# Gram products in three steps with sums of their own, the small chain moved behind them, and layer 3's first chunk prepared at a quarter's end

## The chip, the cores and the metric

The program runs on one core of a Trainium2 chip. A core has five engines with a queue of instructions each: TensorE (PE, matrix products; PEld is its loading of weights), VectorE (DVE), ScalarE (ACT), GpSimd (POOL) and SyncE (SP, which here only issues transfers). Data sits in SBUF (on chip, 128 partitions), products land in PSUM, and transfers (DMA) move tiles from and to memory. The metric is the device time of one execution in microseconds; before the change it is 2779.62 us in the median of three runs (2778.86 to 2781.19).

## The reference, cut to what matters

The input x has 16 images of 64 channels and 128 x 128 pixels. Four layers follow each other. Each normalizes its input by groups of two channels (`_gn`), computes something of it, and adds that to its unnormalized input.

```python
x = x + L0(_gn(x))   # gram = xf xf^T / N of an image; conv_w (gram xf)
x = x + L1(_gn(x))   # |Scharr x| + |Scharr y|, a channel at a time
x = x + L2(_gn(x))   # temporal shift of channels, then a 3x3 convolution and a bias
x = x + L3(_gn(x))   # 3x3 convolution, 1x1 convolution, batch norm over ALL images, leaky relu, clip to 0..255
```

Layer 0 needs the gram matrix of a whole image (64 x 64 sums over 16,384 pixels, and the sums of the channels) before it can give the first pixel. Its result is a single 64 x 64 matrix for each image, by which x is multiplied. The statistics of layer 1's normalization follow from the same gram matrix. Layers 2 and 3 need the mean and variance of the whole image that the layer ahead has made. Layer 3's batch norm needs all 16 images, so the end of the program reads everything once more.

## The kernel before, in words

Two halves of an image (64 rows each) lie on partitions 0 to 63 and 64 to 127, or, from layer 2 on, even and odd rows. An image is worked on in `NS` = 8 chunks of 8 rows, and a chunk of each stage is done in one *step*. The loop at line 1022 goes over steps, and each step over four quarters q = 0 to 3. Every engine works through its queue in the program's order (`InOrder`, line 56), so the order of this Python code is the order of the queues.

Four stages work at the same time, on different images:

- `Gram` (line 458) loads x of an image in eight pieces `xr` (line 493), copies each on ScalarE into the transposed layout `xw` (`rows_to_columns`, line 415), and then has TensorE multiply 128 pairs of columns (`gram_product`, line 406). `xw` has one buffer. For images 7 to 15 the products' sums `pg` lie in a part of `bank`, the PSUM bank that the small products of the chains use as well.
- `gram_chain` (line 303) turns the sums into layer 0's matrix `abd` and into the coefficients `co1` of layer 1's normalization. It is a generator: some sixteen links, alternately small products on TensorE and small operations on VectorE, and two square roots on ScalarE (`sd`). `tick` (line 256) is called at the end of each quarter and advances each open chain by a link. `coefficients` (line 279) is a shorter chain of the same kind, which gives the normalization of layers 2 (`coefs2`) and 3 (`coefs3`).
- `Front` (line 520) does layers 0 and 1: `po` is the product of x with `abd`, `xh` the normalized rows, `u` and `e` the Scharr filters on VectorE, whose absolute values ScalarE takes at the start of quarter 2.
- `Layer2` (line 736) normalizes its chunk `v` in quarter 1 on ScalarE; GpSimd then scales edges and zeroes columns (six instructions); VectorE makes differences `d` of rows, GpSimd issues transfers that copy them into `qd`; TensorE multiplies `one` and `two`. ScalarE copies `one` into `c`.
- `Layer3` (line 884) does the same for layer 3, with `prepare` (line 890) for the normalization. For chunk 0 `prepare` first takes the coefficients, has VectorE make two small factors for the chunk's first and last row (`edge_lower`, `edge_upper`), and then has ScalarE normalize a row with `edge_lower` and the chunk's two halves. Before, it is called in quarter 1 in the stage's own turn (line 941), and that turn is the first of the three stages'.

Image b enters `Front` with chunk 0 in step 15 + 8b, `Layer2` in 25 + 8b, `Layer3` in 35 + 8b. For b = 7 to 15 `Gram` begins at step 8b - 19. Its products were issued in quarters 0 and 2 of step 8b - 11 and in quarter 0 of 8b - 10, 44, 42 and 42 of them. In a steady loop the steps repeat every eight, so the number of a step modulo 8 tells what it holds: chunk 0 of layer 3 is prepared in step 34 + 8b (2 modulo 8), the chain ran from step 6 over 7, 0, 1 to 2.

At the end of each step, in quarter 3, the loop calls `Layer2` once more with "last of 3" (line 1038), where the difference for the next chunk is made. After the loop, a tail reads y and x of all images, applies the batch norm and writes the result.

Of the kernel before, what the change touches and what calls it, by code (L numbers as in the profile page):

```python
# [10 lines left out]
F32 = mybir.dt.float32  # L11
AF = mybir.ActivationFunctionType
ALU = mybir.AluOpType
# [3 lines left out]
P = 128  # L17
# [91 lines left out]
def tile_kernel(ctx: ExitStack, tc: tile.TileContext, x, cw_h, w2_t, b2, wbin_t, w1_t, b1, gamma, beta, consts, out):  # L109
# [141 lines left out]
                    )  # L251


    chains = []

    def tick():
# [45 lines left out]

    def gram_chain(b, pg):

        gs = stp.tile([P, C + 1], F32, tag="gs", name=f"gs_{b}", bufs=1)
        dve.tensor_copy(gs, pg)
        if b > 1:
            yield
        gd = sm(C + 1)
        small_product(gd, k("same"), gs)  # L310
        yield
        g = stp.tile([P, C + 1], F32, tag="g", name=f"g_{b}", bufs=1)
        dve.tensor_scalar_mul(g, gd, 1.0 / HW)
        mu = g[:, C:C + 1]
        st = sv("st0", 2)
        dve.tensor_copy(st[:, 0:1], mu)

        junk0 = stp.tile([P, C], F32, tag="junk0", name=f"junk0_{b}", bufs=1)
        dve.scalar_tensor_tensor(
            junk0, g[:, 0:C], GN_EPS, k("Id"), op0=ALU.add, op1=ALU.mult, accum_out=st[:, 1:2]  # L320
        )
        if b > 1:
            yield
        pm = sm(2)
        small_product(pm, k("gavg"), st)
        yield
        r, me = sv("r"), sv("me", 2)
        yield from rstd(pm, r, me)

        vv = sv("vv", 3)  # L330
        dve.tensor_copy(vv[:, 0:1], mu)
        dve.tensor_sub(vv[:, 1:2], mu, me[:, 0:1])
        dve.tensor_scalar_mul(vv[:, 2:3], me[:, 0:1], -1.0)
        dd = stp.tile([P, 2, C], F32, tag="dd", name=f"dd_{b}", bufs=1)
        for s in range(2):
            dve.tensor_scalar_mul(dd[:, s, :], k("Id"), vv[:, s:s + 1])
        if b > 1:
            yield

        pr = sm(2 * C)  # L340
        small_product(pr, k("all"), dd.rearrange("p s c -> p (s c)"))
        yield

        t0 = stp.tile([P, C], F32, tag="t0", name=f"t0_{b}", bufs=1)
        dve.scalar_tensor_tensor(t0, pr[:, 0:C], vv[:, 0:1], g[:, 0:C], op0=ALU.mult, op1=ALU.subtract)
        cs = stp.tile([P, 2, C], F32, tag="cs", name=f"cs_{b}", bufs=1)
        for s in range(2):
            dve.scalar_tensor_tensor(cs[:, s, :], pr[:, C:2 * C], vv[:, 1:2], t0, op0=ALU.mult, op1=ALU.subtract)
        rc = stp.tile([P, C], F32, tag="rc", name=f"rc_{b}", bufs=1)
        dve.tensor_scalar(rc, cwh, r, 0.5, op0=ALU.mult, op1=ALU.mult)  # L350
        csf = cs.rearrange("p s c -> p (s c)")
        if b > 1:
            yield
        pq = sm(C)
        small_product(pq, csf, rc)
        yield
        r2 = sv("r2")
        dve.tensor_mul(r2, r, r)
        for s in range(2):
            rows = slice(s * C, (s + 1) * C)  # L360
            dve.tensor_scalar_mul(wbd[rows, rows], pq[rows], r2[rows])
        ad = stp.tile([P, C], F32, tag="ad", name=f"ad_{b}", bufs=1)
        dve.scalar_tensor_tensor(ad, pq, r2, k("Id"), op0=ALU.mult, op1=ALU.add)
        abd = stp.tile([P, P], F32, tag="abd", name=f"abd_{b}", bufs=EARLY + 3)
        dve.tensor_add(abd, wbd, k("I"))
        if b > 1:
            yield
        pd = sm(C + 3)
        small_product(pd[:, 0:C], csf, ad)
        small_product(pd[:, C:C + 2], abd, vv[:, 0:2])  # L370
        small_product(pd[:, C + 2:C + 3], wbd, vv[:, 2:3])
        yield
        pp = stp.tile([P, 2, C], F32, tag="pp", name=f"pp_{b}", bufs=1)
        dve.tensor_mul(
            pp, pd[:, 0:C].unsqueeze(1).to_broadcast([P, 2, C]), ad.unsqueeze(1).to_broadcast([P, 2, C])
        )
        av = sv("av", 3)
        dve.tensor_copy(av, pd[:, C:C + 3])
        if b > 1:
            yield  # L380
        pk = sm(1)
        small_product(pk, pp.rearrange("p s c -> p (s c)"), k("q"))
        if b > 1:
            yield
        bias = av[:, 2:3]
        st1 = sv("st1", 2)
        dve.tensor_add(st1[:, 0:1], av[:, 0:1], bias)
        t = sv("t1")
        dve.scalar_tensor_tensor(t, av[:, 1:2], av[:, 1:2], pk, op0=ALU.mult, op1=ALU.subtract)
        dve.scalar_tensor_tensor(  # L390
            st1[:, 1:2], st1[:, 0:1], st1[:, 0:1], t, op0=ALU.mult, op1=ALU.subtract
        )
        if b > 1:
            yield
        pm = sm(2)
        small_product(pm, k("gavg"), st1)
        yield

        co = stp.tile([P, 5], F32, tag="co1", name=f"co1_{b}", bufs=EARLY + 3)
        r, mean = co[:, 0:1], co[:, 3:4]  # L400
        yield from rstd(pm, r, co[:, 3:5], GN_EPS)
        dve.scalar_tensor_tensor(co[:, 1:2], bias, mean, r, op0=ALU.subtract, op1=ALU.mult)
        dve.reciprocal(co[:, 2:3], r)
        lead[b] = abd, co

    def gram_product(pg, w):

        s = w % 2
        pe.matmul(
            pg[s * C:(s + 1) * C, :], xw[:, w // 2, 0:C, s], xw[:, w // 2, :, s],  # L410
            start=(w < 2), stop=(w >= W - 2),
        )
        last[0] = s

# [8 lines left out]
    def first_gram():  # L423
# [13 lines left out]
        for m in range(NS + 1):  # L437
            if m < NS:
                two = ps_two.tile([P, 2, CP, W], F32, tag="two", name=f"turned_{m}").rearrange("p a j w -> p (a j) w")
                for j in range(R):  # L440
                    pe.transpose(two[:, j], src[m][:, j * P:(j + 1) * P], k("I"))
                for h, copy in ((0, dve.tensor_copy), (1, act.copy)):
                    copy(xw[:, m * R:(m + 1) * R, 0:C, h], two[:, :, h * C:(h + 1) * C])
            if m > 0:
                for w in range(2 * R * (m - 1), 2 * R * m):
                    gram_product(pg, w)
        run(Front, 0, Front.first, 0)
        live[Front, 0].load(1)

# [6 lines left out]
                rows_to_columns(1, link - 2, rows[link - 2])  # L456

    class Gram:
        first, last = 0, NS + 1

        def __init__(self, b):
            self.b, self.xr, self.w = b, {}, 0

        def at(self, i, q):
            b = self.b
            if i < NS:
                if q == 0 and i != 1:
                    for m in range(i + (1 if i == 2 else 2) if i else 0, min(i + 3, NS)):
                        self.load(m)

                if q == 3 and i > 0:
                    for m in (0, 1) if i == 1 else (i,):
                        rows_to_columns(b, m, self.xr.pop(m))
                return
            n = 4 * (i - NS) + q

            self.part({0: 44, 2: 42, 4: 42}.get(n, 0))
            if n == 6:
                chains.append(gram_chain(b, self.pg))

        def part(self, n):
            if self.w == 0 and n:
                if self.b <= 2 * EARLY:
                    self.pg = ps_g.tile([P, CP, W], F32, tag="g", name=f"pg_{self.b}")[:, 0, 0:C + 1]
                else:

                    self.pg = bank[:, 3 * P:3 * P + C + 1]
            for _ in range(n // 2):
                for s in (1 - last[0], last[0]):
                    gram_product(self.pg, self.w + s)  # L490
                self.w += 2

        def load(self, m):
# [390 lines left out]
    class Layer3:  # L884
# [37 lines left out]
        def at(self, i, q):  # L922
# [10 lines left out]
            if q == 1:  # L933
                if 0 <= i < NS:
# [2 lines left out]
                    self.v.pop(i)  # L937
                    self.c = ring.tile([P, CP * W], F32, tag="c3", name=f"c3_{b}_{i}", bufs=1)
                    act.activation(self.c, flat(one), AF.Identity, bias=b1_sb)
                if i + 1 < NS:  # L940
                    self.prepare(i + 1)
                if 1 <= i:
                    y = self.y.pop(i - 1)
# [4 lines left out]
            if q == 2:  # L948
                if 0 <= i < NS:
# [5 lines left out]
                        self.c.unsqueeze(1).to_broadcast([P, 2, CP * W]),  # L955
                        op0=ALU.mult, op1=ALU.add, accum_out=bn_sum[:, n:n + 1],
                    )
                if i + 1 < NS:
                    difference("d3", 0, self.v[i + 1])
            if q == 3:  # L960
                if i + 1 < NS:
                    self.twin(0)
                    difference("d3", 1, self.v[i + 1])
                if 0 <= i < NS:
                    act.activation(
                        junk, self.y[i].rearrange("p s j w -> p (s j w)"), AF.Square,
                        accum_out=bn_sq[:, n:n + 1],
                    )
# [51 lines left out]
            fetched[0] += 1  # L1020

    for step in range(starts[2][1] - 2, steps):
        for q in range(4):
            for b in range(B):

# [5 lines left out]
            for stage, at in starts:  # L1031
                if stage is Front and q in (1, 3):
                    issue_rest()
                for b in range(B):
                    run(stage, b, step - at - NS * b, q)
            if q == 3:
                for b in range(B):
                    run(Layer2, b, step - starts[1][1] - NS * b, "last of 3")
            for b in range(1, B):
                at, n = pace[b]  # L1040
                if n == 1:
# [113 lines left out]
```

## Time and profile before

| What | Value |
|---|---|
| Median of three runs | 2779.62 us |
| The profiled execution | 2778.27 us |
| Its span in the profile | 2776.5 us |
| PE busy | 2175.3 us, 78% |
| DVE busy | 2192.0 us, 79% |
| ACT busy | 2112.6 us, 76% |
| POOL busy | 893.2 us, 32% |
| Gram products into `bank` (xw), 2304 matmul rows | 76.5 us |
| Columns, `xw<-xr` on ScalarE, 120 | 139.7 us, 1178 ns each |

Busy time of an engine is the time in which it ran something, not time without which the program would be shorter. "<-" after a row names what ended the idle time before it. In the names, what is written stands left of "<-" and what is read right of it. All instructions that go through `InOrder` carry one line (L73), so groups are told apart by tiles. A float32 matmul appears as two rows of the trace, and a pair that works on both column halves of the array as four. The page cuts the span into forty slices; in the digits 9 means 90% or more.

### The profile page before, as it was taken

Reading aid. Unit: us, or ns where it says so; the run is one execution under the profiler, and the core shown is the slowest. Engines: PE = TensorE matmul, PEld = TensorE weight load, DVE = VectorE, ACT = ScalarE, POOL = GpSimd, SP = SyncE. Lnnn points to the kernel's source line nnn. Section 1 sums busy time; section 2 is a strip of 40 time slices with the busy share of each in tenths; the row PEclk is TensorE's granted clock in tenths of the full one; section 3 lists DMA queues with packets and bytes.
Section 4 is the critical chain, followed back from the end, with each engine's and each line's share of the span. In section 5 each row is a group of like instructions: output and inputs, shape, how many; then the busy total and the mean of one; then the engine's idle time right before and its main releaser. Section 6 shows DMA issues by size and latency. Waiting matters only on the chain. (4 is left out here: it accounts for less than half of the span.)

```text
span 2776.5 us, 46105 instructions
## 1 busy us (share of the span) xinstructions
PE 2175.3 (78%) x14804; PEld 886.4 (32%) x14804; DVE 2192.0 (79%) x3623; ACT 2112.6 (76%) x3177; POOL 893.2 (32%) x1350
## 2 busy tenths in 40 slices
PE   6578899999999999999999999999999994000000
PEld 4233433434343434343433342333334641000000
DVE  4999999898989898989899999999996435333332
ACT  4766889898989898989898988999997667333332
POOL 2055434343434343434343344444444300000000
PEclk8689999999999999999999999999999997555555
DMA  8799888988888888888888777878877768999999
GB/s 205 201 229 238 211 216 226 231 215 229 218 227 213 229 221 221 216 230 216 230 218 227 206 188 197 217 202 219 215 199 195 213 196 288 420 420 420 420 420 384
DMA packets 693601, 685.96 MB, mean 247 GB/s; under 512 B 60096, under 2 KB 580448, under 8 KB 693360
## 3 DMA queue, kind: packets, MB, share of 16 engines
q1 hardware_dynamic: 668208, 613.83, 75.2%
q0 software_dynamic: 25152, 69.18, 10.2%
q8 instruction: 119, 1.95, 0.3%
q14 instruction: 122, 1.00, 0.1%
HBM read 346.23 MB, written 268.44 MB: 221 GB/s over the span
## 5 line engine op out<-in xcount | busy, mean ns | idle before, releaser
L73 PE MATMUL two<-d,w 128*64 128x508 f32 (+2 forms) x2560 | 846.8, 588 | 0.0
L73 PE MATMUL two<-d,wi 128*64 128x508 f32 (+3 forms) x1536 | 578.0, 579 | 0.0
L73 POOL DMA_DIRECT2D qd<-d x512 | 270.8, 531 | 903.7 <-DVE d L73 287.4
L73 PE MATMUL two<-qd,pk 128*64 128x512 f32 (+1 forms) x1024 | 519.0, 588 | 13.3 <-DMA qd<-d 12.5
L73 POOL TENSOR_SCALAR edges<-v,co 64x8 f32<-64x8 f32 x512 | 359.9, 703 | 307.7 <-ACT v L73 231.4
L73 DVE TENSOR_TENSOR d<-v 128x512 f32<-128x512 f32 (+1 forms) x512 | 345.6, 678 | 87.6 <-issue 55.5
L73 PE MATMUL one<-v,w 128*64 128x508 f32 (+2 forms) x1600 | 378.6, 599 | 34.8 <-ACT c L73 34.8
L73 PEld LDWEIGHTS two<-d,w 128*64 128x64 f32 x2560 | 263.1, 136 | 314.9 <-issue 278.5
L73 PE MATMUL one<-v,wi 128*64 128x508 f32 (+3 forms) x1536 | 358.5, 599 | 3.1 <-issue 2.6
L73 ACT COPY qd<-d 64x512 f32<-64x512 f32 x512 | 315.4, 616 | 20.8 <-DVE d L73 14.5
L73 DVE SCALAR_TENSOR_TENSOR e<-e 128x1032 f32<-128x1032 f32 (+1 forms) x256 | 312.9, 1222 | 0.0
L73 ACT ACTIVATE xh<-po,co 128x128 f32<-128x128 f32 (+1 forms) x480 | 275.2, 621 | 31.4 <-PE po L73 22.7
L73 POOL TENSOR_SCALAR v<-v,kc 128x9 f32<-128x9 f32 x256 | 234.6, 930 | 12.0
L73 DVE SCALAR_TENSOR_TENSOR y<-two,c 128x1024 f32<-128x1024 f32 x128 | 155.9, 1218 | 102.8 <-ACT v L73 65.4
L73 PEld LDWEIGHTS two<-d,wi 128*64 128x64 f32 x1536 | 175.6, 136 | 186.0 <-issue 169.6
L73 ACT ACTIVATE v<-x,co 128x512 f32<-128x512 f32 (+2 forms) x368 | 234.9, 705 | 0.0
L73 ACT ACTIVATE u<-u 128x1024 f32<-128x1024 f32 x128 | 135.3, 1057 | 106.8 <-DVE u L73 106.4
L73 PE MATMUL po<-x,abd 64*64 64x512 f32 (+1 forms) x1024 | 178.5, 643 | 44.0 <-ACT xh L73 41.0
L73 PEld LDWEIGHTS one<-v,w 128*64 128x64 f32 x1600 | 126.0, 139 | 237.9 <-issue 162.7
L73 PEld LDWEIGHTS two<-qd,pk 128*64 128x64 f32 x1024 | 136.3, 136 | 153.9 <-issue 110.6
L73 PEld LDWEIGHTS one<-v,wi 128*64 128x64 f32 x1536 | 108.9, 138 | 224.1 <-issue 209.0
L73 DVE SCALAR_TENSOR_TENSOR u<-xh 128x1170 f32<-128x1170 f32 x128 | 175.6, 1371 | 5.1 <-ACT xh L73 4.2
(165 smaller groups left out, 3333.9 us busy)
## 6 DMA issues: line engine op xcount, KB each, us to landing
x<-in_x SPq DMA_DIRECT2D x256, 256.0 KB, 4.1
x_d<-u SPq DMA_DIRECT2D x512, 128.0 KB, 3.8
y_d<-y SPq DMA_DIRECT2D x512, 128.0 KB, 4.0
x_d<-x SPq DMA_DIRECT2D x496, 128.0 KB, 2.6
xr<-in_x SPq DMA_DIRECT2D x120, 512.0 KB, 6.4
qd<-d POOLq DMA_DIRECT2D x256, 130.0 KB, 3.1
qd<-d POOLq DMA_DIRECT2D x256, 129.8 KB, 3.9
v<-x_d SPq DMA_DIRECT2D x448, 72.1 KB, 3.3
```

The costliest lines, as they stand in the source:

```text
L73: return self.tc.keep_in_program_order(call(*args, **kwargs))
```

## The change

Three things are edited.

The gram products of images 7 to 15 are issued in three steps, one block in quarter 1 of each: 44 in step 8b - 11, 42 in 8b - 10, 42 in 8b - 9. Each block has its own accumulation, side by side in `bank` (`first`, `end` and `at`), and the chain adds the three with a `tensor_reduce` where it copied one sum. The columns move with them: they are copied in quarters spread from step 8b - 17 to 8b - 12, with two in some steps, and the load of a later piece follows right behind each column.

The chain of image b, whose first link still takes the sums out of PSUM, then pauses until step 8b - 4 (`now`), and runs from there to step 8b - 1; the next image's products lie in steps 8b - 3 to 8b - 1. The tile `gs`, which holds the sums meanwhile, gets two buffers.

Layer 3's chunk 0 is prepared under "last of 1", after all three stages have had their turn in quarter 1, and its first difference under "last of 2". For this the loop calls `Layer3` and `Layer2` with "last of q" in each quarter. Other chunks stay where they were.

```diff
--- before.py
+++ after.py
@@ -251,6 +251,7 @@
                     )
 
 
+    now = [0]
     chains = []
 
     def tick():
@@ -302,9 +303,14 @@
 
     def gram_chain(b, pg):
 
-        gs = stp.tile([P, C + 1], F32, tag="gs", name=f"gs_{b}", bufs=1)
-        dve.tensor_copy(gs, pg)
+        gs = stp.tile([P, C + 1], F32, tag="gs", name=f"gs_{b}", bufs=2)
+        if b > 2 * EARLY:
+            dve.tensor_reduce(gs, pg.rearrange("p (j c) -> p c j", j=3), axis=AX.X, op=ALU.add)
+        else:
+            dve.tensor_copy(gs, pg)
         if b > 1:
+            yield
+        while b > 2 * EARLY and now[0] < NS * b - 4:
             yield
         gd = sm(C + 1)
         small_product(gd, k("same"), gs)
@@ -403,12 +409,12 @@
         dve.reciprocal(co[:, 2:3], r)
         lead[b] = abd, co
 
-    def gram_product(pg, w):
+    def gram_product(pg, w, first, end):
 
         s = w % 2
         pe.matmul(
             pg[s * C:(s + 1) * C, :], xw[:, w // 2, 0:C, s], xw[:, w // 2, :, s],
-            start=(w < 2), stop=(w >= W - 2),
+            start=(w < first + 2), stop=(w >= end - 2),
         )
         last[0] = s
 
@@ -443,7 +449,7 @@
                     copy(xw[:, m * R:(m + 1) * R, 0:C, h], two[:, :, h * C:(h + 1) * C])
             if m > 0:
                 for w in range(2 * R * (m - 1), 2 * R * m):
-                    gram_product(pg, w)
+                    gram_product(pg, w, 0, W)
         run(Front, 0, Front.first, 0)
         live[Front, 0].load(1)
 
@@ -456,38 +462,43 @@
                 rows_to_columns(1, link - 2, rows[link - 2])
 
     class Gram:
-        first, last = 0, NS + 1
+        first, last = 2, NS + 2
 
         def __init__(self, b):
-            self.b, self.xr, self.w = b, {}, 0
+            self.b, self.xr, self.w, self.parts = b, {}, 0, 0
 
         def at(self, i, q):
             b = self.b
-            if i < NS:
-                if q == 0 and i != 1:
-                    for m in range(i + (1 if i == 2 else 2) if i else 0, min(i + 3, NS)):
-                        self.load(m)
-
-                if q == 3 and i > 0:
-                    for m in (0, 1) if i == 1 else (i,):
-                        rows_to_columns(b, m, self.xr.pop(m))
+            n = 4 * (i - NS) + q
+
+            self.part({1: 44, 5: 42, 9: 42}.get(n, 0))
+            if n == 10:
+                chains.append(gram_chain(b, self.pg))
+
+            if i == 2 and q == 0:
+                for m in range(3):
+                    self.load(m)
+            m = {11: 0, 13: 1, 15: 2, 19: 3, 21: 4, 23: 5, 27: 6, 31: 7}.get(4 * i + q)
+            if m is not None:
+                rows_to_columns(b, m, self.xr.pop(m))
+                if m + 3 < NS:
+                    self.load(m + 3)
+
+        def part(self, n):
+            if not n:
                 return
-            n = 4 * (i - NS) + q
-
-            self.part({0: 44, 2: 42, 4: 42}.get(n, 0))
-            if n == 6:
-                chains.append(gram_chain(b, self.pg))
-
-        def part(self, n):
-            if self.w == 0 and n:
-                if self.b <= 2 * EARLY:
+            first, end, at = 0, W, 0
+            if self.b <= 2 * EARLY:
+                if self.w == 0:
                     self.pg = ps_g.tile([P, CP, W], F32, tag="g", name=f"pg_{self.b}")[:, 0, 0:C + 1]
-                else:
-
-                    self.pg = bank[:, 3 * P:3 * P + C + 1]
+            else:
+
+                self.pg = bank[:, 2 * P:2 * P + 3 * (C + 1)]
+                first, end, at = self.w, self.w + n, self.parts * (C + 1)
+                self.parts += 1
             for _ in range(n // 2):
                 for s in (1 - last[0], last[0]):
-                    gram_product(self.pg, self.w + s)
+                    gram_product(self.pg[:, at:at + C + 1], self.w + s, first, end)
                 self.w += 2
 
         def load(self, m):
@@ -937,7 +948,7 @@
                     self.v.pop(i)
                     self.c = ring.tile([P, CP * W], F32, tag="c3", name=f"c3_{b}_{i}", bufs=1)
                     act.activation(self.c, flat(one), AF.Identity, bias=b1_sb)
-                if i + 1 < NS:
+                if 0 <= i and i + 1 < NS:
                     self.prepare(i + 1)
                 if 1 <= i:
                     y = self.y.pop(i - 1)
@@ -955,8 +966,12 @@
                         self.c.unsqueeze(1).to_broadcast([P, 2, CP * W]),
                         op0=ALU.mult, op1=ALU.add, accum_out=bn_sum[:, n:n + 1],
                     )
-                if i + 1 < NS:
+                if 0 <= i and i + 1 < NS:
                     difference("d3", 0, self.v[i + 1])
+            if q == "last of 1" and i == -1:
+                self.prepare(0)
+            if q == "last of 2" and i == -1:
+                difference("d3", 0, self.v[0])
             if q == 3:
                 if i + 1 < NS:
                     self.twin(0)
@@ -1020,6 +1035,7 @@
             fetched[0] += 1
 
     for step in range(starts[2][1] - 2, steps):
+        now[0] = step
         for q in range(4):
             for b in range(B):
 
@@ -1033,9 +1049,9 @@
                     issue_rest()
                 for b in range(B):
                     run(stage, b, step - at - NS * b, q)
-            if q == 3:
+            for stage, at in starts[:2]:
                 for b in range(B):
-                    run(Layer2, b, step - starts[1][1] - NS * b, "last of 3")
+                    run(stage, b, step - at - NS * b, f"last of {q}")
             for b in range(1, B):
                 at, n = pace[b]
                 if n == 1:
```

## The prediction

> **What bounds the kernel now.** I read the page's engine table and its forty slices first.
>
> ```profile
> PE 2175.3 (78%) x14804; PEld 886.4 (32%) x14804; DVE 2192.0 (79%) x3623; ACT 2112.6 (76%) x3177; POOL 893.2 (32%) x1350
> ...
> DVE  4999999898989898989899999999996435333332
> ...
> PEclk8689999999999999999999999999999997555555
> DMA  8799888988888888888888777878877768999999
> ```
>
> Three engines share the load almost evenly until about 2320 us; then a tail of transfers runs for about 450 us. The change touches nothing in the tail, so only the loop counts. There I cut the trace at every start of VectorE's `u<-xh`, the first instruction of a step; the first of 128 is step 15. I call a step by its number modulo 8, its class. From step 55 to 110 all images repeat to 0.05 us. These are the busy times of one such image, steps 79 to 86, classes 7, 0, 1, 2, 3, 4, 5, 6:
>
> ```profile
> core 0: us, PE busy (x) PEld busy (x) DVE busy (x) ACT busy (x) POOL busy (x), PEclk, DMA share, GB/s
> 1068.20:1086.64 18.44, 18.44 (x102) 6.13 (x100) 17.88 (x49) 17.80 (x28) 7.04 (x12) 1.00 0.88 230
> 1086.64:1103.23 16.59, 16.59 (x125) 8.38 (x123) 16.26 (x30) 14.83 (x24) 5.88 (x10) 1.00 0.91 241
> 1103.23:1120.35 17.12, 15.79 (x93) 6.38 (x91) 16.81 (x31) 15.13 (x25) 7.87 (x11) 1.00 0.92 239
> 1120.35:1137.99 17.64, 14.23 (x70) 4.40 (x68) 16.99 (x35) 13.75 (x24) 5.06 (x9) 0.97 0.88 240
> 1137.99:1152.92 14.93, 14.93 (x70) 4.61 (x68) 14.56 (x20) 14.81 (x23) 7.01 (x11) 0.92 0.73 188
> 1152.92:1167.84 14.92, 14.92 (x76) 4.81 (x74) 14.55 (x20) 14.82 (x24) 7.37 (x11) 1.00 0.75 198
> 1167.84:1187.14 19.30, 19.30 (x244) 9.73 (x241) 14.66 (x21) 18.00 (x29) 5.00 (x10) 1.00 0.97 237
> 1187.14:1204.81 17.67, 17.67 (x163) 7.56 (x161) 14.76 (x21) 12.73 (x21) 5.42 (x10) 1.00 0.74 188
> sum 136.61, PE 131.87 PEld 52.00 DVE 126.47 ACT 121.88 POOL 50.66; mean PE 16.48 PEld 6.50 DVE 15.81 ACT 15.23 POOL 6.33
> ```
>
> In classes 7, 0, 1 and 2 VectorE works nearly without a break: the chain lies there. In classes 5 and 6 TensorE bounds: gram products lie there, and VectorE idles 4.64 and 2.91 us. The same cut of a late image (steps 119 to 126), with neither products nor chain, gives the base:
>
> ```profile
> 1790.90:1807.11 16.21, 15.54 (x78) 4.78 (x76) 15.66 (x26) 13.91 (x23) 7.86 (x10) 1.00 0.82 218
> ...
> sum 122.34, PE 121.67 PEld 42.86 DVE 120.18 ACT 113.17 POOL 59.01; mean PE 15.21 PEld 5.36 DVE 15.02 ACT 14.15 POOL 7.38
> ```
>
> So products, columns and chain cost 14.3 us an image, while VectorE's share of them is only 6.3. That difference is what balance could win. The waits and ScalarE's timeline of step 82 (class 2) show the place of the third edit:
>
> ```profile
> PE one L73 <- ACT c L73: 2.3, 1, 2.3
> ACT v L73 <- DVE edge_lower L73: 1.8, 1, 1.8
> ```
> ```profile
> 1126.32 0.49 ACT L73 ACTIVATE v<-x,edge_lower 128x128 f32<-128x128 f32 x1 [1.76 <-DVE edge_lower L73]
> 1126.72 1.50 ACT L73 ACTIVATE v<-x,co 128x512 f32<-128x512 f32 x2
> 1128.13 1.34 ACT L73 ACTIVATE v<-v,co 128x1154 f32<-128x1154 f32 x1
> 1131.52 0.20 ACT L73 ACTIVATE sd<-nv 128x1 f32<-128x1 f32 x1 [2.05 <-DVE nv L73]
> 1131.63 1.04 ACT L73 ACTIVATE u<-u 128x1024 f32<-128x1024 f32 x1
> ```
>
> ScalarE waits for the edge factors, then normalizes layer 3's chunk, then layer 2's (`v<-v`), and only then takes the Sobel absolute values (`u<-u`).
>
> **What the skill says.** The Trainium skill, "TensorE: Matmul & The Clock Gate", section "Architectural detail", calls ScalarE and VectorE strict first-in first-out queues. The trace agrees: in the 1.76 us before `edge_lower` ScalarE ran nothing, though `v<-v` stood behind. "PSUM — Partial Sum Buffer", "The four PSUM rules", says that two accumulation groups open in one bank and quadrant can't both begin with a clearing matmul; this is why products that interleave with an earlier chain in the same bank need three sums. No run here shows it yet. "SBUF — State Buffer", section "SBUF: two separate sides", has VectorE and GpSimd exclude each other on a shared port. The trace fits: GpSimd's six instructions after `v<-v` take 3.99 us in step 82 and 6.34 in step 122.
>
> **Part 1, products.** Matmul count is unchanged. A block of 42 products holds TensorE 2.6 us, 44 hold it 2.75 (from its last neighbour before to the next after, step 85). Without products a step costs TensorE 14.85 (start of `one<-v,w` in step 124 to that in 126, less 0.2 for `pe`). Before: both 2.75 and 2.6 in class 5, 2.6 in class 6. Now 5, 6, 7 hold one each, about 17.5 a step with switches (step 86, from one `one` to the next). Adding three sums of 65 costs VectorE 0.36 instead of 0.22 us, by the slope between the reduces of 16 and 128 elements (162 and 286 ns): 1 us in all.
>
> **Part 2, chain.** It had 2.69 us of VectorE instructions nominally in class 7, 2.4 in class 0, 1.0 in 1, 1.6 in 2; net of overlap I use the measured differences to the plain image (1.87, 1.92, 0.66, 1.33). Now it starts in class 4 by the step counter and takes sixteen quarters: 1.0 in class 4 (`g`, `st`, `junk`, first `me`, `nv`), 2.1 in class 5, 1.45 in 6, and 0.45 + 0.5 + 1.0 in 7. No instruction is added, but products of the next image share the bank and wait for VectorE's last reader of it, which is 2 us or more earlier in each class: free.
>
> **Part 3, columns and loads.** Eight copies of 1.15 us on ScalarE an image, two fewer in class 6, one fewer in 5 and more in 0 and 2 (one of them between layer 3's chunk and the absolute values). Each load of 512 KB (0.57 us on SP) now stands right behind its column, so SP waits for ScalarE there, with the x load (2 issues), stores of u (4), y (4) and loads of v (6) behind it, some 10 us of issuing. Even in class 3, where SP starts 2.8 us late, v's loads are issued by about 13.5 us and needed 7 us into the next step: free; about 1 us a step if not.
>
> **Part 4, layer 3's first chunk.** Edge factors now stand behind VectorE's four Sobel instructions. By step 122: final coefficients end at 5.7 us into the step, Sobel 4.57, factor 0.25: ScalarE may start at 10.54, where it began at 5.97. Then 1.81 for the three activations, 1.1 for the column, 1.06 for the absolute value: VectorE's `u<-xh,co,u` can start at 14.55, but is reached at 11.7. It stalls 2.85 us; without a column 1.75. What is gained: `v<-v` is early, so the 0.23 us wait for GpSimd goes.
>
> **Sum, by class, for an image with products.** The time is VectorE's base plus chain plus stalls.
> - 0: 14.5 (was 16.6). 1: 16.6 (was 17.1), with 0.2 for a late `v<-v` after two columns in class 0.
> - 2: 16.2 - 0.25 + 2.85 = 18.8 (was 17.65).
> - 3: ScalarE is late; `v<-v` ends at 9.85 instead of 8.73, GpSimd's 5.4 (its usual in class 3) end at 15.3, `d<-v` of layer 2 waits from 14.04: 15.95 (was 14.93).
> - 4: 14.65 + 1.0 = 15.65 (was 14.92).
> - 5: 14.65 + 2.1 = 16.75 (was 19.3): TensorE, 0.8 us ahead, needs 18.1 and is 0.6 behind at the end.
> - 6: VectorE's `d<-v` may overwrite only when layer 2's first half has read it: 16.0 us after `one<-v,w` in a step with one block (step 86: 1.06 to 17.06), so 0.6 + 16.0 + 0.35 for the chain's matmuls; plus 0.6: 17.5 (was 17.7).
> - 7: TensorE enters 0.95 behind; `d<-v` at 17.15 (VectorE is there at 15.9), then 0.46 and 2.35 of coefficients: 19.95 (was 18.43).
>
> Sum 135.7 against 136.6: 0.9 us less. Seven whole images, steps 55 to 110: -6.3. Steps 39 to 54, with the first products and no chain yet: +1.7 - 0.9. Steps 111 to 118: +3.0, since the last chain now falls into steps 116 to 119 with no products to cover it. Steps 119 to 126: +3.9 (2.1 chain, 1.5 and 0.3 for the layer 3 chunk). Steps 127 to 142: 2 x 1.8. Step 34: +1.3. Together +6.3 us. On the profiled execution's 2778.27 (span 2776.5) this is 2784.6; on the runs' median of 2779.62 it is 2786.
>
> **Rivals.**
> - Balance without the hold (faster). TensorE is idle over 4 us at the end of class 2; if it enters class 5 ahead by 2.2 us rather than 0.8, the holds of 1.4 in class 6 and 1.2 in class 7 shrink or go: up to 2.6 x 9 = 23 us off the sum, 2763. Against it: `one` has a single buffer, so it can't start before ScalarE's `c`, and after its wait in step 82 it lost another 1.4 us at a lower clock (0.92 in class 3). It decides from about 1 us of extra lead.
> - Layer 3's chunk is free (faster): 3.85 x 9 + 1.9 x 5 = 44 us off, 2742. The order of both queues speaks against it.
> - ScalarE's lateness carries on (slower). After class 2 it is 2.7 us late and has 14.8 us of work a step with a column against VectorE's 14.65; if it stalls classes 3 and 4 by 1.5 us more each, 9 x 3 = 27 on top: 2813. Class 4's spare chain time speaks against it.
>
> **How the numbers follow.** My sum 0.48, give or take 12 us; the lead 0.25; the free chunk 0.07; carried lateness 0.2. The first three lie within 2740 to 2800, so 2752 to 2813 holds eight in ten; the likeliest alone gives 2774 to 2798. A measurement here tells 0.2% (5.6 us) from no change: faster means under 2774, slower over 2785. Faster: 0.25 and 0.07 nearly whole, with a little of my sum, 0.32; slower: half of my sum and the last rival, 0.46; same 0.22.
>
> **What would show it.** VectorE idle before `u<-xh,co,u` of about 2.85 us in class 2, released by ScalarE's `u`, 1.75 in late images; class 5 near 16.75 and class 0 near 14.5; class 7 near 20 with `d<-v` waiting for TensorE. A step of class 2 under 17 us, or class 7 under 18.7, would prove the sum wrong, as would SP queues that delay layer 2's `v`.

## The result and the profile after

The changed kernel takes 2797.67 us in the median (2795.71 to 2798.33), beside 2780.4 for the kernel before in the same job: a ratio of 1.0061, 95% interval 1.0043 to 1.0078. It is 17 us slower, where I had forecast 6. My 2786 lies some 12 us under the measured time; the side was right and the time lies inside my range of 2752 to 2813, but the size was nearly three times the one I gave.

The page of the changed kernel, engine table and slices, shows next to nothing of it. VectorE (DVE) has 2194.2 us of work where it had 2192.0:

```profile
PE 2180.6 (78%) x14804; PEld 898.5 (32%) x14804; DVE 2194.2 (78%) x3623; ACT 2110.5 (75%) x3177; POOL 935.7 (33%) x1350
...
DVE  4999899899999999999999999999996435333332
```

The same image as in the prediction, cut at the starts of `u<-xh` (steps 79 to 86, classes 7, 0, 1, 2, 3, 4, 5, 6), has its columns as before: the stretch and its length, busy time and instructions of each engine, the granted TensorE clock, DMA:

```profile
1074.39:1094.42 20.03, 20.03 (x182) 8.51 (x180) 18.11 (x47) 16.84 (x28) 8.57 (x12) 1.00 0.94 240
1094.42:1108.90 14.48, 14.48 (x111) 7.20 (x109) 14.34 (x22) 13.07 (x20) 7.34 (x8) 1.00 0.86 235
1108.90:1125.60 16.70, 16.70 (x86) 7.10 (x84) 16.20 (x27) 16.60 (x27) 7.14 (x11) 1.00 0.94 263
1125.60:1144.15 18.55, 13.65 (x66) 4.13 (x64) 15.58 (x27) 13.80 (x22) 6.96 (x10) 0.92 0.87 244
1144.15:1159.81 15.66, 15.66 (x69) 4.70 (x67) 14.57 (x20) 15.54 (x26) 6.72 (x11) 0.88 0.79 211
1159.81:1175.41 15.60, 15.60 (x86) 5.14 (x84) 15.38 (x27) 15.51 (x24) 4.67 (x12) 1.00 0.78 208
1175.41:1192.71 17.30, 17.30 (x165) 7.57 (x163) 16.50 (x34) 15.42 (x26) 7.38 (x10) 1.00 0.70 189
1192.71:1210.89 18.18, 18.18 (x180) 8.25 (x178) 15.95 (x28) 15.05 (x25) 7.68 (x10) 1.00 0.69 182
sum 136.50, PE 131.60 PEld 52.60 DVE 126.64 ACT 121.84 POOL 56.47; mean PE 16.45 PEld 6.58 DVE 15.83 ACT 15.23 POOL 7.06
```

The balance did what it says: the class with two blocks of products, 19.30 us long, has gone to 17.30, and class 0, freed of the chain, from 16.59 to 14.48. Yet the sum is 136.50 where it was 136.61, since classes 2, 3, 4, 6 and 7 took nearly all of it back. The waits in step 82 (class 2) name the place of the layer 3 chunk, and ScalarE's (ACT) and VectorE's timelines of that step show how it passes from queue to queue:

```profile
PE one L73 <- ACT c L73: 4.9, 1, 4.9
ACT v L73 <- DVE edge_lower L73: 4.7, 1, 4.7
...
DVE u L73 <- ACT u L73: 2.7, 1, 2.7
```
```profile
1136.02 0.49 ACT L73 ACTIVATE v<-x,edge_lower 128x128 f32<-128x128 f32 x1 [4.69 <-DVE edge_lower L73]
1136.42 1.50 ACT L73 ACTIVATE v<-x,co 128x512 f32<-128x512 f32 x2
1137.83 1.14 ACT L73 COPY xw<-xr 128x1024 f32<-128x1024 f32 x1
1138.85 1.05 ACT L73 ACTIVATE u<-u 128x1024 f32<-128x1024 f32 x1
```
```profile
1135.76 0.22 DVE L73 TENSOR_SCALAR edge_lower<-co,kc 128x2 f32<-128x2 f32 x1
...
1139.93 1.29 DVE L73 SCALAR_TENSOR_TENSOR u<-xh,co,u 128x1024 f32<-128x1024 f32 x1 [2.69 <-ACT u L73]
```

The factor comes behind the Sobel instructions (the filters `u` and `e` on VectorE), ScalarE waits 4.69 us for it, does three activations and a column, and hands VectorE its absolute values 2.69 us late. ScalarE's `c` is late too, so TensorE stands for 4.90 us. Here is what it does next (its timeline from the end of class 2): twelve rows of `one`, layer 3's first product of the next step, in 5.01 us.

```profile
1143.52 5.01 PE L73 MATMUL one<-v,w 128*64 128x512 f32 x12 [4.90 <-ACT c L73]
```

### The profile page after: what moved, and what is told of

Its sections match the earlier page's. It is cut to its first block, busy times and chain, and to the rows that moved or that the text cites. A ratio compares the mean times of both kernels' runs of the same rounds, so it can differ in the third digit from the quotient of the medians.

```text
span 2796.2 us, 46087 instructions
## 1 busy us (share of the span) xinstructions
PE 2180.6 (78%) x14804; PEld 898.5 (32%) x14804; DVE 2194.2 (78%) x3623; ACT 2110.5 (75%) x3177; POOL 935.7 (33%) x1350
## 5 line engine op out<-in xcount | busy, mean ns | idle before, releaser
L73 PE MATMUL two<-d,w 128*64 128x508 f32 (+2 forms) x2560 | 838.4, 587 | 0.0
L73 POOL TENSOR_SCALAR edges<-v,co 64x8 f32<-64x8 f32 x512 | 408.5, 798 | 280.6 <-ACT v L73 158.4
L73 PE MATMUL one<-v,w 128*64 128x508 f32 (+2 forms) x1600 | 389.0, 613 | 58.1 <-ACT c L73 58.1
L73 POOL TENSOR_SCALAR v<-v,kc 128x9 f32<-128x9 f32 x256 | 228.3, 905 | 11.9
L73 PEld LDWEIGHTS one<-v,w 128*64 128x64 f32 x1600 | 132.3, 143 | 264.3 <-issue 170.6
L73 DVE SCALAR_TENSOR_TENSOR u<-xh,co,u 128x1024 f32<-128x1024 f32 x128 | 164.4, 1284 | 35.3 <-ACT u L73 35.3
```

The lines of the kernel that those rows point to most:

```text
L73: return self.tc.keep_in_program_order(call(*args, **kwargs))
```

## The experiments

Each kernel was timed in three rounds against the kernel before. None leaves out any work.

**1. The balance without the late chunk.** Theory: the late chunk costs far more than it shows in class 2 alone, and the balance is a gain. Rival: lateness only takes the place of waits for TensorE that come anyway.

```diff
-                if 0 <= i and i + 1 < NS:
+                if i + 1 < NS:
                     self.prepare(i + 1)
...
-            if q == "last of 1" and i == -1:
-                self.prepare(0)
-            if q == "last of 2" and i == -1:
-                difference("d3", 0, self.v[0])
```

> The changed kernel with its third edit undone: layer 3's chunk 0 is prepared in its turn again. My theory: the late chunk costs VectorE's 2.69 us wait in class 2, about 0.9 us in class 3 and a little more in the images without products, so this gives back some 40 us of the changed kernel's 2798: about 2757, with class 2 near 16.3 us. Rival (the lateness only takes the place of waits for TensorE that come anyway): classes 5 to 7 grow by as much as 2 and 3 shrink, and it stays above 2785.

Measured: 2737.78 us, ratio 0.9856 (0.9841 to 0.987). The rival falls, and my own number was 19 us too high. The same eight steps of this kernel (classes 2 to 6 and the sum):

```profile
1095.93:1112.14 16.21, 14.70 (x72) 4.42 (x70) 15.67 (x27) 14.67 (x24) 7.86 (x10) 1.00 0.91 242
1112.14:1127.07 14.93, 14.93 (x76) 4.54 (x74) 14.56 (x20) 14.81 (x24) 7.01 (x11) 1.00 0.92 266
1127.07:1142.67 15.60, 15.60 (x86) 5.15 (x84) 15.38 (x27) 15.51 (x24) 4.79 (x12) 1.00 0.84 213
1142.67:1159.36 16.69, 16.69 (x167) 7.39 (x164) 16.40 (x33) 15.19 (x26) 7.51 (x10) 1.00 0.86 221
1159.36:1175.93 16.57, 16.57 (x165) 7.30 (x163) 15.95 (x27) 14.66 (x24) 7.70 (x10) 1.00 0.69 179
sum 131.20, PE 129.69 PEld 51.70 DVE 126.61 ACT 121.55 POOL 57.92; mean PE 16.21 PEld 6.46 DVE 15.83 ACT 15.19 POOL 7.24
```

Class by class against the changed kernel, the late chunk costs 2.34 us in class 2, 0.73 in class 3, nothing in class 4, but again 0.61 in class 5 and 1.61 in class 6, three and four steps after its cause. How it gets there is told by TensorE's timeline. In this kernel, `one` of class 3 takes 2.78 us, and class 5 (which begins at 1142.67) is entered 1.88 us ahead:

```profile
1110.69 2.78 PE L73 MATMUL one<-v,w 128*64 128x512 f32 x12 [0.29 <-ACT c L73]
...
1140.79 2.73 PE L73 MATMUL one<-v,w 128*64 128x512 f32 x12
```

In the changed kernel the same twelve rows take 5.01 us after the wait, and TensorE enters class 5 (at 1175.41) 0.33 us late:

```profile
1175.74 2.73 PE L73 MATMUL one<-v,w 128*64 128x512 f32 x12
```

The granted clock (the third figure from the end) tells why the rows are slow. It is 0.55 over them in the changed kernel (first line) and 1.00 here, and 2.78 / 0.55 is 5.05:

```profile
1143.52:1148.53 5.01, 5.01 (x14) 1.62 (x16) 4.86 (x10) 4.92 (x8) 1.29 (x3) 0.55 1.00 270
1110.69:1113.47 2.78, 2.78 (x14) 1.06 (x16) 2.56 (x5) 2.75 (x5) 1.76 (x3) 1.00 0.66 185
```

The 5.01 - 2.78 = 2.23 us lost at the low clock are about the missing lead, 1.88 + 0.33 = 2.21. Counted from the start of class 7 (1074.39 and 1044.73), TensorE reaches class 5 5.29 us later in the changed kernel, and its image is 5.30 us longer: the two classes that TensorE bounds pass on all that it had lost by then.

**2. The late chunk alone, on the kernel before.** It is the same edit without the balance.

> The kernel before with the third edit alone. My theory: there part of the new wait hides behind the chain's own VectorE work in class 2, but not in the five images without products: 15 to 25 us slower, about 2800, class 2 near 18.2 us with products and 17.5 without. Rival (the edit helps, since layer 2's chunk is normalized earlier): 2770 to 2778.

Measured: 2808.63 us, ratio 1.011 (1.0095 to 1.0125), 30 us slower; somewhat more than expected. In class 2 the chain that still lies there hides part (1.0 us of wait where the changed kernel has 2.7); without products class 2 takes 17.52 us, as expected. But class 5, which has two blocks of products here, grows from 19.30 to 20.17 us in half of the images. Classes 2 and 5 of such an image:

```profile
1138.12:1156.76 18.64, 14.12 (x70) 4.25 (x68) 17.00 (x35) 13.59 (x24) 6.52 (x9) 0.93 0.86 234
1186.89:1207.06 20.17, 20.17 (x247) 10.03 (x245) 14.63 (x20) 17.98 (x29) 4.81 (x10) 1.00 0.94 233
```

What sets the halves apart is the clock. Going into step 75 (class 3), `one` took 4.47 us; TensorE then entered class 5 (at 1048.90) on time, and the class took 19.37 us, about as in the kernel before. Going into step 83, `one` took 5.36 us; TensorE entered class 5 (at 1186.89) 0.78 us late, and the class took 20.17:

```profile
1017.41 4.47 PE L73 MATMUL one<-v,w 128*64 128x512 f32 x12 [4.74 <-ACT c L73]
1048.86 2.73 PE L73 MATMUL one<-v,w 128*64 128x512 f32 x12
...
1155.11 5.36 PE L73 MATMUL one<-v,w 128*64 128x512 f32 x12 [4.52 <-ACT c L73]
1187.67 2.73 PE L73 MATMUL one<-v,w 128*64 128x512 f32 x12
```

The granted clock over `one` is 0.62 in the first and 0.50 in the second. Of the eight images from step 47 to 110, four are of each kind (19.22 to 19.37 us, and 20.16 to 20.17). Their instructions are the same, and in all of them `one` begins 1.65 us before its step, so this shows the path from clock to lead to class 5 apart from any edit.

The edit is a loss by itself, on both schedules.

**3. Early factors, late activations.** Which of the two orders is at fault, the factors' in VectorE's queue or the activations' in ScalarE's? Only the two small factors go back ahead of the Sobel instructions.

```diff
+        def factors(self):
+            self.co = coefs3.pop(self.b)
+            self.edge = {}
+            for half in ("lower", "upper"):
+                self.edge[half] = sv(f"edge_{half}", 2)
+                dve.tensor_scalar_mul(self.edge[half], self.co, k(half))
...
+                if i == -1:
+                    self.factors()
                 if 0 <= i and i + 1 < NS:
                     self.prepare(i + 1)
```

> The changed kernel, but the two edge factors are made in layer 3's turn, ahead of the Sobel instructions, while the activations stay late. My theory (the factors' place in VectorE's queue is the cause): the 4.7 us wait of ScalarE in class 2 goes, class 2 is near 16.2 us and the whole near 2755. Rival (the late activations themselves delay the absolute values): class 2 stays above 17.5 us and the whole above 2785.

Measured: 2733.16 us, ratio 0.9838 (0.9822 to 0.9855). With the factors early the loss is gone, and more than that: their place in VectorE's queue is the cause, and the activations' place in ScalarE's is not. ScalarE's timeline of step 82 now reads as the edit may have been meant: layer 2's chunk first, then 0.23 us of wait, and `u<-u` waits for VectorE instead of the other way round:

```profile
1099.14 1.35 ACT L73 ACTIVATE v<-v,co 128x1154 f32<-128x1154 f32 x1
1100.72 0.49 ACT L73 ACTIVATE v<-x,edge_lower 128x128 f32<-128x128 f32 x1 [0.23 <-DVE edge_lower L73]
1101.12 1.51 ACT L73 ACTIVATE v<-x,co 128x512 f32<-128x512 f32 x2
1102.53 1.17 ACT L73 COPY xw<-xr 128x1024 f32<-128x1024 f32 x1
1104.27 1.06 ACT L73 ACTIVATE u<-u 128x1024 f32<-128x1024 f32 x1 [0.57 <-DVE u L73]
```

With the factors early, late activations are even worth 4.6 us against experiment 1: class 2 is 15.91 us, and the wait for GpSimd is gone. In time they are not late at all. They start 5.98 us into the step, and 5.97 in experiment 1; layer 2's chunk fills the 1.48 us that ScalarE waited there for the factor. So two VectorE instructions of 0.22 us each, four instructions too late in their queue, cost 2797.67 - 2733.16 = 64 us (from two jobs, in which the kernel before took 2780.4 and 2778.43 us).

**4. The products back in two steps, the chain still paused.**

```diff
-            self.part({1: 44, 5: 42, 9: 42}.get(n, 0))
-            if n == 10:
+            self.part({0: 44, 2: 42, 4: 42}.get(n, 0))
+            if n == 6:
```

> The changed kernel with the products in the two steps where they were before (still three sums), the chain still paused, the chunk still late. My theory: TensorE has the same work in classes 5 to 7 and sets the end there either way; class 5 goes to about 20 us, class 7 falls to about 18.5 us, and the whole is within 5 us of the changed kernel, about 2795. Rival (the block in class 7 costs by itself, since VectorE's coefficients stand behind it): class 7 falls and class 5 doesn't grow as much, 2783 or less.

Measured: 2817.89 us, ratio 1.0146 (1.0131 to 1.0161). Both expectations failed: class 7 falls to 18.37 us as expected, but class 5 grows to 21.4 to 21.7. VectorE's timeline of step 85 there, with TensorE's below it:

```profile
1208.15 0.28 DVE L73 SCALAR_TENSOR_TENSOR t<-bank,vv,g 128x64 f32<-128x64 f32 x1 [4.60 <-PE bank L73]
```
```profile
1200.74 0.44 PE L73 MATMUL bank<-dd,kc 128*64 128x128 f32 x4
1205.30 2.81 PE L73 MATMUL bank<-xw 128*64 128x65 f32 x84
```

The product that the chain wants (`bank<-dd`) is done by about 1201.2. Its reader starts 7 us later, within 0.04 us of the end of a block of gram products (1208.11) that writes other columns of the same bank. So the program's wait covers the whole bank: a reader whose turn comes after a block waits for that block. In the changed kernel each block lies in quarter 1 *ahead* of the chain's product, so nothing of this shows there. The prediction priced only the other direction, blocks that wait for VectorE's readers. The Trainium skill, "PSUM — Partial Sum Buffer", section "PSUM bank collisions raise a hardware error", advises to guard PSUM by bank and quadrant, not by address; 4.60 us is what a guard by bank costs in this step, where two streams share one bank.

**5. No pause, chunk in its turn.** The pause is taken out of experiment 1, which splits the balance into its two parts.

```diff
-        while b > 2 * EARLY and now[0] < NS * b - 4:
-            yield
```

> The changed kernel with layer 3's chunk in its turn and with no pause in the chain, which then follows the products through classes 0 to 3. It splits the balance into its two edits. My theory: the chain's 6 us of VectorE work then falls on classes that VectorE already sets (0 to 3), and classes 5 and 6, which TensorE sets, gain little: some 3.4 us an image, about 2768. Rival (spreading the products alone makes the gain): it stays at 2738.

Measured: 2763.74 us, ratio 0.9942 (0.9925 to 0.9958), near the 2768 expected; an image takes 134.58 us, 3.38 more than in experiment 1, where I had 3.4. Products in three steps, with their columns, gain 16 us alone (2779.58 to 2763.74), the pause another 26 (2763.74 to 2737.78), and the late chunk takes 60 (to 2797.67). The last two differences go across jobs, between which the kernel before moved by up to 2 us.

**6. The third block at the end of class 7.** Class 7 is still 20 us long in every kernel with both a block and the chain there (20.03 in the changed kernel, 20.02 in experiment 1, 20.03 in experiment 3). In the changed kernel VectorE waits 1.28 us before the difference `d<-v`, with the coefficients queued behind:

```profile
1091.60 0.56 DVE L73 TENSOR_TENSOR d<-v 128x384 f32<-128x384 f32 x1 [1.28 <-issue]
```

The trace names no releaser here ("issue"); that it is layer 2's products is what this run is to show. On top of experiment 3, the block moves behind layer 2's products.

```diff
-        first, last = 2, NS + 2
+        first, last = 2, NS + 3
...
-            self.part({1: 44, 5: 42, 9: 42}.get(n, 0))
-            if n == 10:
+            self.part({1: 44, 5: 42, 11: 42}.get(n, 0))
+            if n == 12:
...
-            m = {11: 0, 13: 1, 15: 2, 19: 3, 21: 4, 23: 5, 27: 6, 31: 7}.get(4 * i + q)
+            m = {12: 0, 13: 1, 15: 2, 19: 3, 21: 4, 23: 5, 27: 6, 31: 7}.get(4 * i + q)
```

> The kernel with early factors and late activations, and in class 7 the third block of products moved from quarter 1 to the end of quarter 3, the sums taken in quarter 0 of class 0, and the next image's first column copied there too. My theory: class 7 is 20.0 us because VectorE's difference waits 1.3 us for layer 2's products behind the block, with coefficients queued behind it; then class 7 falls by 1.3 us, class 0 takes the block without loss, and nine images give 12 us: about 2721. Rival (TensorE's work is the bound there in any order): class 0 or 1 grows by as much, and it stays within 3 us of 2733.

Measured: 2720.1 us, ratio 0.9786 (0.9771 to 0.98). Classes 7 and 0 of this kernel:

```profile
1036.15:1054.54 18.39, 18.39 (x166) 7.79 (x164) 17.75 (x46) 16.01 (x29) 8.57 (x12) 1.00 1.01 249
1054.54:1069.29 14.75, 14.75 (x111) 6.57 (x107) 14.61 (x23) 14.16 (x21) 6.96 (x8) 1.00 0.90 229
```

Class 7 gives back 1.64 us and class 0 takes 0.26. The wait before `d<-v` is gone from class 7, which is 1.28 of the 1.64; the rest is the adding of the sums, 0.35 us of VectorE, which is done in class 0 now. So the wait in class 7 was the order on TensorE, not its load. (A column moved to class 0 as well; ScalarE had room in class 7, 17.11 us busy of 20.03 in experiment 3.) The kernel is the fastest here, 60 us below the kernel before.

## Why the prediction was right or wrong

| Class | Before | Predicted | After |
|---|---|---|---|
| 7 | 18.44 | 19.95 | 20.03 |
| 0 | 16.59 | 14.5 | 14.48 |
| 1 | 17.12 | 16.6 | 16.70 |
| 2 | 17.64 | 18.8 | 18.55 |
| 3 | 14.93 | 15.95 | 15.66 |
| 4 | 14.92 | 15.65 | 15.60 |
| 5 | 19.30 | 16.75 | 17.30 |
| 6 | 17.67 | 17.5 | 18.18 |
| Sum | 136.61 | 135.7 | 136.50 |

- **Parts 1 and 2, products and chain:** right. Each class moved the way the sum had it, but for class 6, which was to lose 0.2 us and gained 0.5 (by the lead, below), and VectorE's work stayed equal (126.47 and 126.64 us an image).
- **Part 4, the late chunk:** the mechanism was right to the step. The stall was put at 2.85 us with a column and 1.75 without; the trace has 2.69 in step 82 and 1.66 in step 122. GpSimd's delay in class 3 was put at 1.3, and is 0.94.
- **The mis-sized term, TensorE's lead into class 5.** I let TensorE enter class 5 0.8 us ahead, having taken over the 1.4 us that it lost at a low clock in the kernel before. After the late chunk it lost 5.01 - 2.78 = 2.2 us, and entered 0.33 us late. The missing 1.1 us came back as 0.55 in class 5 and 0.68 in class 6. Classes 2 and 3 had been put 0.54 us too high together, which hid part of it. With it the seven whole images gained 1.3 us (the sum of steps 55 to 110, by the starts of `u<-xh`) in place of 6.3.
- **Step 34 was put at 1.3 us and costs 3.5.** It prepares the first image's chunk, when no `y` of an earlier image stands between the factors and `u<-xh,co,u`, and a column is copied there too: VectorE's wait is 3.87 us. My 1.3 is near the 1.5 that I gave a late image, where a `y` does stand between and no column is copied. Steps 31 to 38 together cost 4.4, steps 23 to 30 0.7 (not in the sum at all).
- **Other stretches:** steps 39 to 54 cost 2.0 us (0.8 predicted), 111 to 118 cost 4.3 (3.0 predicted), 119 to 126 4.4 (3.9), 127 to 142 3.65 (3.6). The kernel's span grew by 19.7 us, of which 18.15 lie ahead of step 142; the other 1.6 lie in the last step and the tail, and their cause stays open.
- **Part 3:** columns and loads cost nothing that shows, apart from the column in class 2, which the sum had under Part 4 (a stall of 2.69 us with it, 1.66 without). Class 1, with the late `v<-v`, was put at 16.6 and is 16.70.
- **The rivals:** TensorE's lead did decide, but with the opposite sign: it shrank. Experiment 1 shows that the rival's mechanism is real: with 1.88 us of lead VectorE's wait in class 6 falls from 1.93 to 0.32 us, though the one in class 7 stays (1.29). "The chunk is free" fell. Lateness of ScalarE was carried on, as the third rival had it, but by way of TensorE's clock and lead rather than as stalls in classes 3 and 4.

For the late chunk as a whole, I had put the price at 3.85 us an image; it is 136.50 - 131.20 = 5.3. Over the program I had 44 us for it and 2742 us without it, which makes the balance worth 38. Experiment 1, without it, took 2737.78: the balance gains 41 us (within one job), and the late chunk costs some 58 to 60. So the balance was sized nearly right, a little low, and the miss is the late chunk's price.

## What to carry to other kernels

When an instruction is moved back in one queue, ask what small instruction on another engine it needs, and whether that moved back as well: here two factors of 0.22 us behind four long Sobel instructions cost some 64 us, while the same activations at the same late place in the queue are a gain with the factors early. Where several engines are nearly full, a stall is not paid where it stands: follow each engine's lead into the stage that it bounds. An edit made of several parts is worth splitting even when its sum is small; this one held a gain of some 41 us and a loss of some 58 to 60.

## What the runs showed of the hardware

- After a wait of 4.90 us TensorE ran twelve rows of `one` in 5.01 us at a granted clock of 0.55, against 2.78 us at 1.00 after a wait of 0.29. The Trainium skill, "TensorE: Matmul & The Clock Gate", section "HAM oscillation", warns of idle gaps beyond some 3.4 us, and the trace agrees. In step 82 of the kernel before, though, waits of 1.09 and 2.33 us, 1.9 us apart, were already followed by 4.48 us at 0.62, while in step 122 of experiment 1 a single wait of 2.31 us was followed by 2.78 us at 1.00.
- How much is lost does not follow from the length of the wait: in experiment 2 a wait of 4.52 us was followed by 5.36 us of `one`, and one of 4.74 by 4.47. What decides it stays open.
- A read of one region of a PSUM bank waited until a block of products into another region of it had ended (4.60 us in experiment 4). That is the program's own guard, not shown to be the chip's.
